# Four graph layers on 32 batches: attention rows spread by DMA through DRAM, and an unmasked attention written as products of exponentials

## The chip, the core and the metric

One core of one Trainium2 chip runs the whole kernel. Its engines are named as in the profile: PE (TensorE, matrix products and transposes), DVE (VectorE), ACT (ScalarE), POOL (GpSimd), SP (SyncE, which here issues nearly all DMAs). PEld is PE's weight load. The metric is the device time of one execution in microseconds (us); the kernel before took 4562.52 us, the median of three runs (4557.34 to 4564.04).

## What is computed

The input x has 32 batches (here called graphs) of 512 nodes with 256 channels, all in float32, and one 512x512 adjacency matrix that they share. Four layers follow each other; each normalizes, applies a ReLU and adds its result to x:

```
h = max(layernorm(x), 0); x = x + L0(h)   # MLP, GAT without a mask, MLP, GAT with the mask
h = max(layernorm(x), 0); x = x + L1(h)   # GAT with the mask and its own node
h = max(layernorm(x), 0); x = x + L2(h)   # transformer block, 8 heads, masked
h = max(layernorm(x), 0); x = x + L3(h)   # GAT with 4 heads, masked

gat(inp, mask, W, a):
    h  = inp @ W
    f1 = h @ a[:F];  f2 = h @ a[F:]
    e  = leaky_relu(f1[:, None] + f2[None, :], 0.2)
    e  = where(mask > 0, e, -9e15)            # left out where there is no mask
    return elu(softmax(e, axis=2) @ h)
```

So there are seven GAT attentions per graph: one without a mask (layer 0, first), and six with it (layer 0, second; layer 1; four heads in layer 3). The change is about how their 512x512 probabilities are made.

## The kernel before

**Tiles.** Nodes or channels lie on 128 partitions; NC = 4 blocks of 128 nodes make 512. A "cell" buffer holds 128 x 1044 floats in SBUF, a "row" buffer 128 x 522, a "page" is a 128 x 1024 buffer in DRAM, a "bank" one of the eight PSUM banks of 128 x 512. "Smalls" are columns of a few floats per partition, one tile for each of the IN_FLIGHT = 6 graphs that may be under way together. There are 31 cells, 9 rows and 72 pages (BUFFERS, L47).

**Attention with a mask** (`gat_probabilities`, L631). The probabilities stand transposed: source node j on the partitions, target node i along the row. `terms` gives each node f2, (1 - alpha) f1 and (alpha - 1) f2. First `rows_ps` (L611, transposes at L617) spreads f2 over all partitions: four PE transposes of a column that is broadcast to 128x128, into one bank. DVE takes from it the largest allowed f2 of each target (four operations, L652). POOL makes of that a shift per target, four small operations at L668 to L674. This shift is a column (node on the partition), and is needed as a row (node along the row, the same on all partitions). `row_of` (L622) does that: four PE transposes into a bank (L617) and a copy on ACT into a row buffer, which also scales it (L627). Two POOL operations add the mask and the shift row into the two cells of p (L687), PE spreads the f1 term (L617 again), four DVE operations join it (L699) and four ACT operations take the exponential (L707).

**Attention without a mask** goes through the same function with no bias: one reduction on DVE (L646), a shift on POOL, `row_of`, no mask addition, four DVE operations that read the shift row (L699), four exponentials (L707). Its sums come from POOL (L1003, L1007) and PE (L1013), their reciprocals from DVE (L1020). `row_of` spreads the reciprocals too (L1021), and DVE multiplies the product of PE (L1030) by that row (L1039).

**Layer 2** turns its probabilities on DVE in 32x32 blocks (L1253) and sends them through DRAM for the rest: a store into a page (L1265) and four loads that put the blocks in their places (L1273), before PE multiplies them (L1286). x and some intermediates are parked in pages as well (L836, fetched at L844).

**The order.** All graphs' operations are written down as a list with an engine, a length in us, a lag (time from the engine's end to the result) and the buffers that they read and write. `Plan.order` (L196) then plays them through on a model of the engines: at each step it takes, on the engine that can start first, the operation with the earliest due time. The due time comes from the graph's number times PERIOD, the operation's distance from the graph's end, and a table of hand-set corrections per operation, SHIFTS (L55 to L85). CLOSE draws the last graphs together. A buffer is taken when the first operation that uses it is placed. The instructions are issued in the resulting order, and each engine, SP among them, runs its own in that order and waits at each for its data. So a waiting DMA issue on SP holds up all DMAs behind it.

Of the kernel before, what the change touches and what calls it, by code (L numbers as in the profile page):

```python
# [16 lines left out]
P = 128  # L17
# [19 lines left out]
TERMS = 3  # L37

# [8 lines left out]
BUFFERS = {"cell": 31, "row": 9, "page": 72}  # L47
# [4 lines left out]
PERIOD = 45.2  # L52
CLOSE = 0.92

SHIFTS = (  # L55
    29, -53, -1, -8, -39, -20, -9, 0, -8, 38, 23, -9, -18, -3, -77, -3, -7, -6, -13, -10, -13,
    -33, -38, -26, -19, -7, -80, -68, -33, -44, 32, -52, -73, -3, -2, -3, -5, -2, 6, -30, 6, 5,
    5, 6, -4, 18, 6, 6, 14, -63, 10, 19, 5, -16, 9, -56, 6, -55, 13, 6, 40, -19, 6, 6, 1, 5, 90,
    5, 5, -152, 3, 44, 5, 5, 1, 0, 1, -19, 1, 0, 0, -2, 0, 0, 2, -104, 0, -1, -24, 0, 8, 77,
    -63, 0, -5, 0, 0, 0, -56, -7, -8, -6, -81, -21, 0, 0, 0, 10, -7, -106, 0, 7, 0, 9, -123, 0,  # L60
    -75, 0, 24, 0, -2, 0, -30, 0, 10, -2, -57, -2, 12, -19, 14, -77, -14, -13, -7, -60, -14,
    -89, 11, 70, -25, 40, 115, 21, -17, -2, 9, 4, -46, -116, -40, -40, -73, -57, -135, -92,
    -106, -76, -169, -150, -145, -58, -212, -66, 3, 3, 3, 3, 3, 25, -13, 80, -111, -19, -25, 5,
    4, 4, 22, 4, 6, 72, 4, 13, -112, 49, -50, -12, 23, 59, 66, 91, 75, 21, -152, 167, 58, 23,
    135, 193, 95, -29, 13, 32, -60, -13, 0, -18, 0, 0, 3, 0, 0, -68, 2, 0, 36, -43, 1, -2, -1,
    0, -5, -11, -7, -6, -51, 3, -5, -60, 0, 23, 0, 27, -104, -73, -114, -225, -216, -123, -155,
    -154, -174, -43, -66, -60, 63, 1, -54, -50, 115, 173, -23, 3, 4, -44, 2, -74, 5, 2, -11,
    -36, 3, -26, -3, 2, 2, -43, 2, 2, -147, 2, 2, -18, 2, 0, 11, -144, 0, 22, 0, 68, 0, 120,
    135, 208, 167, 59, 133, 180, 143, 191, 181, 68, 180, 282, 216, 51, 187, 137, 27, 38, -36,
    -29, -50, -5, 0, -56, -9, 0, -36, 0, 0, 0, 2, 0, -37, -34, -12, -7, 79, -5, 0, 21, -117, 0,  # L70
    -4, -9, 1, -7, 1, -27, 1, -43, 7, -146, -60, -60, -61, 12, -35, -122, -200, -73, -9, -31,
# [279 lines left out]
def adj_preln_kernel(  # L351
# [117 lines left out]
    def held(what, which):  # L469
        return [(what, which)]  # L470
# [10 lines left out]
    class Graph:  # L481
# [140 lines left out]
        def row_of(self, holder, col, dst=(), scale=1.0):  # L622
# [5 lines left out]
            )  # L628
            return r

        def gat_probabilities(self, holder, term, n, bias=None, biasT=None, own=False, after=()):  # L631

# [885 lines left out]
```

## Time and profile before

| what | value |
|---|---|
| median of three runs | 4562.52 us (4557.34 to 4564.04) |
| the profiled execution's own time | 4556.81 us |
| its span, first to last instruction | 4555.0 us |
| instructions in the trace | 72980 |
| mean granted clock of TensorE | 0.974 |
| DMAs: packets, volume, mean rate | 481462, 800.41 MB, 176 GB/s |
| DMA landing, median: 128 KB page load (L1273) | 4.1 us |
| the same, 512 KB page store (L1265, L836) | 3.9 us |
| the same, 512 KB page load (L844) | 5.0 us |
| ACT's first column load at the start (512 elements of 4 B, L410) | 4.7 us |

The page gives each engine's busy time and its share of the span. A group's row names the line, the engine, the operation, what it writes and reads, its form and count, then the busy time in us, the mean length of one in ns, the idle time of the engine just before these instructions, and what ended most of that idle time. Matrix instructions of PE overlap, so the length of one is more than the step from one to the next. A float32 product appears as two instructions; a transpose as one. A view of waits names the waiting engine and line, what it waited for, the total in us, how often, and the longest.

### The profile page before, as it was taken

The numbers are of one execution on the slowest core, as the hardware profiler recorded it, in microseconds if no ns is written. First come the engines' busy times: TensorE is split into PE (matmuls) and PEld (weight loads), VectorE is DVE, ScalarE is ACT, GpSimd is POOL, SyncE is SP. The second block draws the span as 40 slices with busy tenths as digits, with TensorE's granted clock in tenths as the row PEclk, the third lists the DMA queues.
The fourth block names the chain that finished last, engine by engine and source line by source line (L and its number), as shares of the span: only waits on it lengthen the run. The fifth ranks groups of instructions, "written<-read, shape, count | busy, mean of one in ns | idle before, by whom it ended". The sixth has DMA issues, their size and how long they took to land. (4 is left out here: it accounts for less than half of the span.)

```text
span 4555.0 us, 72980 instructions
## 1 busy us (share of the span) xinstructions
PE 4328.2 (95%) x22288; PEld 2698.2 (59%) x22288; DVE 3570.2 (78%) x8824; ACT 3110.0 (68%) x6501; POOL 2992.2 (66%) x3055
## 2 busy tenths in 40 slices
PE   8999999999999999999999999999999999999865
PEld 5666666566666566566566666666665656565432
DVE  4576888787888787888887888788788877888864
ACT  4566677677677677677677677777776676677653
POOL 2334766766776766776766776766776666667768
PEclk9999999999999999999999999999999999999977
DMA  3365656555656555656555656555565565565760
GB/s 108 98 190 182 206 168 198 181 176 167 198 182 185 180 182 163 197 182 184 181 183 164 196 185 190 180 187 161 190 194 173 179 194 177 158 198 191 218 184 19
DMA packets 481462, 800.41 MB, mean 176 GB/s; under 512 B 50608, under 2 KB 364464, under 8 KB 481072
## 3 DMA queue, kind: packets, MB, share of 16 engines
q1 hardware_dynamic: 479456, 795.74, 56.3%
q8 instruction: 180, 2.95, 0.3%
q14 instruction: 210, 1.72, 0.1%
q10 hardware_dynamic: 1616, 0.01, 0.0%
HBM read 409.67 MB, written 385.88 MB: 175 GB/s over the span
## 5 line engine op out<-in xcount | busy, mean ns | idle before, releaser
L1243 ACT ACTIVATE cell<-cell,smalls 128x512 f32<-128x512 f32 x1024 | 732.6, 716 | 302.9 <-DVE smalls L1235 293.6
L687 POOL TENSOR_TENSOR cell<-mask_biasT,row 128x1024 f32<-128x1024 bf16 x320 | 683.7, 2149 | 259.6 <-ACT row L627 239.1
L1235 DVE CUSTOM_DVE_ANT_0 cell<-bank,mask_bias 128x512 f32<-128x512 f32 x1024 | 683.4, 674 | 124.8 <-PE bank L1216 121.7
L1253 DVE STREAM_TRANSPOSE cell<-cell 128x512 f32<-128x512 f32 x1024 | 696.8, 696 | 43.8 <-ACT cell L1243 34.5
L652 DVE CUSTOM_DVE_ANT_0 masked<-bank,mask_bias 128x512 f32<-128x512 f32 x768 | 520.5, 678 | 88.4 <-PE bank L617 80.0
L707 ACT ACTIVATE cell<-cell,smalls 128x512 f32<-128x512 f32 x640 | 440.3, 716 | 102.9 <-DVE cell L699 99.7
L794 PE MATMUL bank<-cell,cell 128*128 128x260 f32 x2048 | 478.1, 385 | 4.7 <-ACT cell L707 3.3
L580 PE MATMUL bank<-cell,mlp_sb 128*128 128x512 f32 x1024 | 469.0, 596 | 4.1 <-DVE cell L1168 1.4
L601 PE MATMUL bank<-fc_sb,cell 128*128 128x256 f32 (+1 forms) x2048 | 471.4, 381 | 1.3 <-DVE cell L1077 1.3
L537 ACT ACTIVATE cell<-cell,smalls 128x256 f32<-128x256 f32 x768 | 421.9, 591 | 67.9 <-POOL smalls L530 57.3
L1030 PE MATMUL bank<-cell,cell 128*128 128x512 f32 x1024 | 464.6, 599 | 2.9 <-DVE smalls L1235 2.9
L794 PEld LDWEIGHTS bank<-cell,cell 128*128 128x128 f32 x2048 | 383.8, 190 | 121.8 <-issue 32.6
L601 PEld LDWEIGHTS bank<-fc_sb,cell 128*128 128x128 f32 x2048 | 381.0, 189 | 82.1 <-DVE cell L813 15.9
L1286 PE MATMUL bank<-cell,cell 128*32 128x256 f32 x4096 | 329.0, 423 | 97.0 <-DMA cell<-page 61.2
L617 PEld LDWEIGHTS bank<-ident,smalls 128*128 128x128 f32 x2304 | 266.6, 139 | 215.4 <-issue 62.7
L699 DVE SCALAR_TENSOR_TENSOR cell<-bank,smalls,cell 128x512 f32<-128x512 f32 x512 | 363.4, 737 | 30.5 <-POOL cell L687 29.5
L520 DVE BATCH_NORM_STATS2 smalls<-cell 128x6 f32<-128x256 f32 x768 | 315.1, 410 | 77.0 <-POOL cell L1093 55.1
L617 PE MATMUL bank<-ident,smalls 128*128 128x128 f32 x2304 | 346.5, 281 | 29.0 <-POOL smalls L674 21.1
L763 DVE SCALAR_TENSOR_TENSOR cell<-cell,cell 128x512 f32<-128x512 f32 (+1 forms) x256 | 261.7, 1023 | 136.7 <-ACT cell L754 68.7
L1356 POOL TENSOR_TENSOR cell<-cell,cell 128x1024 f32<-128x1024 f32 x128 | 302.1, 2369 | 84.2 <-DMA page<-cell 24.8
L1046 POOL TENSOR_TENSOR cell<-cell,cell 128x1024 f32<-128x1024 f32 x64 | 151.7, 2370 | 294.4 <-DVE cell L763 166.4
L1093 POOL TENSOR_TENSOR cell<-cell,cell 128x512 f32<-128x512 f32 x192 | 244.1, 1278 | 130.7 <-DMA cell<-page 48.5
(135 smaller groups left out, 8579.3 us busy)
## 6 DMA issues: line engine op xcount, KB each, us to landing
page<-cell SPq DMA_DIRECT2D x704, 512.0 KB, 3.9
cell<-page SPq DMA_DIRECT2D x2048, 128.0 KB, 4.1
cell<-page SPq DMA_DIRECT2D x192, 512.0 KB, 5.0
cell<-in_x_dram SPq DMA_DIRECT2D x64, 512.0 KB, 5.0
out_dram<-cell SPq DMA_DIRECT2D x32, 512.0 KB, 3.0
mlp_sb<-in_L_gnn_mlp_w_dram SPq DMA_DIRECT2D x2, 512.0 KB, 6.4
fc_sb<-in_L_gnn_W_fc_dram SPq DMA_DIRECT2D x1, 1024.0 KB, 6.2
row<-in_adj_dram SPq DMA_DIRECT2D x4, 256.0 KB, 7.0
```

Of the source, the lines that this page charges most:

```text
L537: lambda c=c: act.activation(xn[:, c, :], src[:, c, :], func, bias=off[:, c : c + 1], scale=rstd[:, c : c + 1],),
L580: lambda k=k, s=s, i=i, m=m, mm=mm: pe.matmul(mm.ap, w[:, k, cols + m * P : cols + (m + 1) * P], s[:, i, :], start=(k == 0), stop=(k == nk ...
L601: pe.matmul(mm[:, :n], src[k // 2][:, k % 2, c * P : (c + 1) * P], w[:, k, cols : cols + n], start=(k == 0), stop=(k == nk - 1),)
L617: pe.transpose(bc[:, c * P : (c + 1) * P], col(c).to_broadcast([P, P]), ident)
L652: lambda c=c: dve.tensor_tensor_reduce(masked, f2_ps.ap, bias[:, c, :], 1.0 - ALPHA, FLOOR, op0=ALU.add, op1=ALU.max, accum_out=top[:, c : ...
L687: lambda half=half: pool.tensor_add(p[half].ap, biasT[:, 2 * half : 2 * half + 2, :], w_row[:, None, :].to_broadcast([P, 2, N]),),
L707: lambda j=j, ph=ph, i=i: act.activation(ph[:, i, :], ph[:, i, :], AF.Exp, bias=term(0)[:, j : j + 1]),
L794: pe.matmul(mm[:, :w1], p[j // 2][:, j % 2, c * P : (c + 1) * P], v[:, j, :], start=(j == 0), stop=(j == NC - 1),)
L1030: pe.matmul(mm.ap, h1[jh][:, i, m * P : (m + 1) * P], p[jh][:, i, :], start=(jh + i == 0), stop=(jh + i == 2),)
L1235: lambda h=h, c=c, sc=sc, p=p: dve.tensor_tensor_reduce(p[h // 2][:, h % 2, :], sc[h].ap, mask_bias[:, c, :], -MHA_SCALE, HIGHEST, op0=ALU ...
L1243: lambda h=h, c=c, p=p: act.activation(p[h // 2][:, h % 2, :], p[h // 2][:, h % 2, :], AF.Exp, scale=-1.0, bias=low[:, c, h : h + 1], accu ...
L1253: lambda h=h, c=c, p=p, turned=turned: dve.transpose(turned[h][:, :, :, c % 2, :].rearrange("p l j i -> p j l i"), p[h // 2][:, h % 2, :]. ...
```

## The change

Four things change together.

1. `row_of` is replaced by `row_by_dma`: the column of 128x4 is stored from SBUF into a line of 512 floats in DRAM (one of 32 new "line" buffers), 4 bytes per element, and a second DMA loads this line into all 128 partitions of a row buffer. Both are issued by SP, the second waits for the first to land. It is used for the six masked shifts and for the reciprocals of the open attention. The scale that ACT applied is now applied by POOL to the small column.
2. The attention without a mask no longer adds and then takes exponentials of 128x512. With the lowest term as a reference, three small exponentials (a, e, g) are taken per node, and each probability is, up to a factor per target that the softmax cancels, max(a_i * e_j, g_j): a is spread by PE, and four DVE operations with two scalars each make p. The exponent of a is capped at 40.
3. The planner's lags of DMAs rise (3.4 to 4.2, 3.8 to 4.5), with 5.0 and 4.0 for the two new ones.
4. There are 30 cells instead of 31 and 11 rows instead of 9, and PERIOD, CLOSE and the whole table SHIFTS have other values, so that the order of the instructions on every engine is another one. The planner itself is unchanged.

```diff
-BUFFERS = {"cell": 31, "row": 9, "page": 72}
+BUFFERS = {"cell": 30, "row": 11, "page": 72, "line": 32}
...
-PERIOD = 45.2
-CLOSE = 0.92
+PERIOD = 56.4
+CLOSE = 0.87
 
 SHIFTS = (
...
-        def row_of(self, holder, col, dst=(), scale=1.0):
+        def row_by_dma(self, src, dst=()):
             r = Buffer("row", N)
-            bc = self.rows_ps([holder], col, (), [r, *dst])
-            self.op(
-                "act", 0.6, [bc], [r],
-                lambda: act.activation(r.ap, bc.ap, AF.Copy, scale=scale),
+            line = Buffer("line", N)
+            self.op(
+                "sp", 0.45, [src], [line],
+                lambda: nc.sync.dma_start(
+                    line.ap.rearrange("o (c p) -> p (o c)", p=P), src.ap
+                ),
+                lag=5.0,
+            )
+            self.op(
+                "sp", 0.45, [line], [r, *dst],
+                lambda: nc.sync.dma_start(
+                    r.ap,
+                    bass.AP(tensor=line.ap.tensor, offset=line.ap.offset, ap=[[0, P], [1, N]]),
+                ),
+                lag=4.0,
             )
             return r
 
+        def open_probabilities(self, f):
+            low_ps = self.rows_ps([f], lambda c: f[:, c : c + 1, 2])
+            low = self.small("low", 1)
...
+                lambda: dve.tensor_reduce(
+                    low.ap, low_ps.ap, axis=mybir.AxisListType.X, op=ALU.min
+                ),
...
+                dve.tensor_scalar(
+                    a.ap, f[:, :, 1], low[:, :1], MOST, op0=ALU.subtract, op1=ALU.min
+                )
+                dve.tensor_scalar(d.ap, f[:, :, 2], low[:, :1], None, op0=ALU.subtract)
...
+                act.activation(a.ap, a.ap, AF.Exp)
+                act.activation(e.ap, d.ap, AF.Exp, scale=-1.0 / (1.0 - ALPHA))
+                act.activation(g.ap, d.ap, AF.Exp, scale=-ALPHA / (1.0 - ALPHA))
...
+            p = [Buffer("cell", 2, N) for _ in range(2)]
+            a_ps = self.rows_ps([a], lambda c: a[:, c : c + 1], [e, g], [q for q in p])
+            for j in range(NC):
...
+                    lambda j=j, ph=ph, i=i: dve.tensor_scalar(
+                        ph[:, i, :], a_ps.ap, e[:, j : j + 1], g[:, j : j + 1],
+                        op0=ALU.mult, op1=ALU.max,
+                    ),
...
                 pool.tensor_add(w.ap, t, term(1))
-                pool.tensor_scalar(
-                    w.ap, w.ap, 0.0, (1.0 - ALPHA) / ALPHA, op0=ALU.max, op1=ALU.mult
-                )
+                pool.tensor_scalar(w.ap, w.ap, 0.0, -1.0, op0=ALU.max, op1=ALU.mult)
+                pool.tensor_scalar(t, t, -ALPHA / (1.0 - ALPHA), None, op0=ALU.mult)
                 pool.tensor_add(w.ap, w.ap, t)
...
-            w_row = self.row_of(w, lambda c: w[:, c : c + 1], p, -ALPHA / (1.0 - ALPHA))
+            w_row = self.row_by_dma(w)
...
-            p, _ = self.gat_probabilities([f], lambda t: f[:, :, t], 0)
+            p = self.open_probabilities(f)
...
-            rinv_row = self.row_of(rinv, lambda c: rinv[:, c : c + 1])
+            rinv_row = self.row_by_dma(rinv)
```

## The prediction

> **What bounds the kernel now.** I read the busy shares first, then the span by stages, then who waits for whom, and last the rows of the operations that go.
>
> ```profile
> PE 4328.2 (95%) x22288; PEld 2698.2 (59%) x22288; DVE 3570.2 (78%) x8824; ACT 3110.0 (68%) x6501; POOL 2992.2 (66%) x3055
> ...
> q1 hardware_dynamic: 479456, 795.74, 56.3%
> ```
>
> TensorE (PE) is busy 95% of the span; the next engine, VectorE (DVE), 78%. The view by windows (columns: length, then busy time of PE, weight loads, DVE, ACT, POOL, granted clock, DMA share, GB/s) shows where PE idles:
>
> ```profile
> 2000.00:3000.00 1000.00, 979.48 (x5138) 616.27 (x5136) 819.06 (x2012) 714.73 (x1497) 685.51 (x698) 0.99 0.58 181
> ...
> 4214.00:4328.00 114.00, 94.57 (x528) 49.95 (x528) 97.58 (x253) 76.30 (x170) 85.51 (x78) 0.91 0.72 218
> 4328.00:4442.00 114.00, 76.20 (x387) 42.75 (x386) 75.47 (x190) 57.70 (x130) 77.78 (x78) 0.79 0.63 183
> 4442.00:4555.00 113.00, 63.32 (x229) 32.33 (x227) 50.68 (x110) 43.24 (x74) 90.42 (x78) 0.73 0.06 19
> ```
>
> In the middle PE idles about 20 us in 1000. In the last 341 us (the drain, where the last graphs run out) it idles 107 us and POOL leads at the end. So up to 4214 us the time is PE's instruction stream: what leaves PE there leaves the time, if the other engines still feed it. PE's own waits, and SP's (the queue of all these DMAs):
>
> ```profile
> PE bank L1286 <- DMA cell<-page: 61.2, 42, 3.1
> PE bank L617 <- POOL smalls L674: 21.1, 12, 4.2
> ...
> SPq L1273 <- DMA page<-cell: 410.9, 222, 5.4
> ```
>
> PE waits little for any one thing; the most for pages that layer 2 sends through DRAM. Then the operations that go or slow down:
>
> ```profile
> L617 PE MATMUL bank<-ident,smalls 128*128 128x128 f32 x2304 | 346.5, 281 | 29.0 <-POOL smalls L674 21.1 <-DVE smalls L1020 3.2 <-DVE smalls L652 2.4
> L627 ACT ACTIVATE row<-bank 128x512 f32<-128x512 f32 x256 | 151.2, 592 | 91.7 <-PE bank L617 88.9
> L687 POOL TENSOR_TENSOR cell<-mask_biasT,row 128x1024 f32<-128x1024 bf16 x320 | 683.7, 2149 | 259.6 <-ACT row L627 239.1 <-DMA cell<-page 8.7 <-DVE cell L1039 6.7
> ```
>
> and, from the timeline of PE, a run of eight transposes and a run of four:
>
> ```profile
> 1000.18 1.04 PE L617 MATMUL bank<-ident,smalls 128*128 128x128 f32 x8
> ...
> 1100.59 0.60 PE L617 MATMUL bank<-ident,smalls 128*128 128x128 f32 x4
> ```
>
> **Step 1, PE.** The built order holds 1280 transposes from smalls at this line where it held 2304: 1024 fewer (per graph: four for each of six masked shift rows, four for the reciprocal row, four for the open attention's shift). A transpose's own 281 ns overlaps its neighbours; in the stream, four more cost 1.04 - 0.60 = 0.44 us, 0.11 each. The page's row gives 346.5/2304 = 0.15, neighbours included. I take 0.12, nearer the run: 1024 x 0.12 = 123 us (113 to 154). Of PE's busy time 234 of 4328 us lies in the drain, where PE doesn't set the end, so 94.6% counts: **-116 us** (-107 to -146). The Trainium skill ("TensorE: Matmul & The Clock Gate", Part 4: PE-mode transpose) puts a 128x128 transpose in one kernel's context at about 275 ns, which agrees with the row's 281; used as a price per transpose it would make 282 us. The two timeline rows show that this is a latency, and not the step.
>
> **Step 2, a wait that goes.** PE waited 21.1 us for shifts from POOL (L674) and 3.2 us for the reciprocals (L1020), to spread them. Both instructions are gone. What stands behind them may be late next, so I take half: **-12 us** (0 to -24).
>
> **Step 3, ACT, DVE, POOL.** ACT loses 256 copies (151 us) and 128 exponentials of 716 ns (92 us), and gains 96 of 128x4 (the 128x12 row took 180 ns: 17 us). DVE keeps 128 operations of 128x512 from PSUM in the open attention (730 ns before; two scalars in place of a row), and gains 64 of 128x4 (at 180 ns, the 128x4 reciprocal: 12 us). POOL gains 64 of 128x4 (some 240 ns: 15 us). None sets the middle: 0, hidden under PE, which has over 160 us in 1000 more work than DVE.
>
> **Step 4, the rows' new path.** Before: four transposes and a copy, 0.6 + 0.59 us, 1.3 with the hops. After: a store of 512 elements of 4 B to DRAM and a broadcast load of 256 KB. No row here stores 4 B elements. The nearest is the first column load (512 elements of 4 B from DRAM, on ACT's queue): 4.7 us to landing; the 512 KB page stores take 3.9, and the slowest DMA of the start-up 9.3. I take 4.7, the same count of elements. The load lies between the 128 KB (4.1) and 512 KB rows (5.0): 4.4. Together 9.1 us, 8 more than before. The Trainium skill ("DMA: Bandwidth & Descriptors", Rules for kernel authors) speaks against the store: a last dimension that isn't contiguous becomes one descriptor per element, and should be rearranged. It gives no price for this; the column load agrees that such a transfer is slow for its 2 KB, no run shows the store, and by the rule at its worst the sum is that of the rival on SP below.
>
> The consumer is POOL's mask addition (L687), and behind it on POOL stand the other additions. In the new order the POOL work between a shift and its addition adds up, by the rows' durations, to under 9.5 us for 105 of 192 rows, 463 us short in all; POOL idles 1563 us. Before, POOL idled 249 us for these rows, and PE's weight loads waited 8.2 + 4.1 + 2.8 = 15 us for L687. In proportion 15 x 463/249 = 28: **+13 us**. Ends: 0 (POOL's idle time hides it), and +79, if the 92.1 us that DVE waited for L687 grow alike and all reach PE. The reciprocal rows are covered: between reciprocal and first use the new order has some 16 us of DVE work (8 before), short of 9.5 us once.
>
> **Step 5, SP and the DMA engines.** SP issues 448 more DMAs, at some 0.4 us 180 us; it issues for about 1240 us of 4555 now, so this hides. The wait that is added is the load's for its store, with all of SP's queue behind it. In the new order 86 of 224 pairs have no more than one issue between, so SP stands still there. Directly behind the 224 loads stand another shift's DMA 106 times, layer 2's pages 77 times, and parked x pages. But the same order moves layer 2's own stores and loads apart: 14 of 512 have at most one issue between where 139 had, 7.3 on average where it was 4.1. So 100 close pairs stand where 139 stood. The DMA engines get busier: 28,672 packets of 2 KB at the mean 86 ns of a packet (56.3% x 16 x 4555/479,456) are 3.4% of the span, and 114,688 of 4 B between 1.4% (9 ns, the packet time of the column loads in the trace) and 13.5% (86 ns): from 56% to 61-73%. PE's waits for pages at L1286 are 61.2 us, 87 with the weight loads'. Wider spacing and busier engines pull opposite ways: **0**, between -87 (all gone) and +87 (doubled).
>
> **Step 6, the drain.** The last addition of layer 1 (own mask) starts at 4231.5 us, so the drain holds little but layers 2 and 3. Layer 3's first row is 8 us later, the other heads' rows come while POOL works: **+8 us** (0 to +16, two graphs).
>
> **Sum.** -116 - 12 + 13 + 0 + 8 = -107: span 4555 - 107 = 4448; with the 1.8 us around it (4556.8 measured) 4450; the median of the runs stands 5.7 us above the profiled one: **4455 us**.
>
> **Rivals.** (a) *SP becomes the bound: slower.* Now 411 us of SP's waiting for page stores go with 87 us of PE's waiting for pages, 0.21 to one. The 107 us gained are used up by 510 us more of SP's waiting: 2.3 us per pair if all 224 wait, 5.9 if only the 86 close ones do. So it decides from a store that lands after 7 to 10.6 us rather than 4.7. At 11 us and all pairs: 224 x 6.3 x 0.21 = 296 us, 4750; the close ones alone: 114, 4570; between, **4660**. For: nothing here shows the store, and single page loads took 8.8 us. Against: the column loads' 4.7. (b) *The other engines take half back.* DVE has 819 us of 1000; on a span shorter by 2.5% 840, in order, with ACT waiting 294 us for it (L1243 <- L1235). If PE's idle time in the middle grows from 22 to 35 us in 1000: 13 x 3.9 = 50, **4505**. For: buffers fall from 31 to 30. Against: ACT is freed of 226 us. (c) *The new order mends pages and drain too:* half of the 87, and a third of the drain's 107 us: 4455 - 43 - 36 = **4376**. That the change does not do what it says is excluded for the counts by the built order.
>
> **How the numbers follow.** About 0.2% (9 us) is what a measurement here can tell from no change. Forecast (4400 to 4505) 0.60; (b) (4505 to 4553) 0.17; (c) and below 0.07; so faster 0.84; same 0.05; (a) and like it, slower, 0.11. The steps' ends, taken as independent, reach 94 us down (30, 12, 13, 87, 8 squared and added) and 111 up (9, 12, 66, 87, 8): 4361 to 4566. 8 in 10 lie within **4365 to 4550**, leaving some 0.04 below, 0.16 above.
>
> **What would show it.** Step 1: some 1800 transposes in place of 2816 in all, PE busy near 4205, PE share still about 94-95%. Step 2: no PE wait for L674. Step 4: line<-smalls landing near 4.7 us and row<-line near 4.4, POOL waiting some 460 us for rows. Step 5: PE's wait at layer 2's product (L1286) near 87 us, DMA share 61-73%. Step 6: PE idle in the last 341 us near 115. I am wrong if the stores land after 7 us and PE's waits for pages grow past 190 us (rival a), if PE's share falls under 93.5% in the middle with DVE or ACT behind its waits (rival b), or if the transposes' step was not 0.12 us.

## The result, and the profile after

The changed kernel took 5977.02 us (median of four runs, 5950.70 to 5983.38), the kernel before on the same chip 4560.27 (4557.34 to 4564.04). The ratio is 1.3095 (95% interval 1.3054 to 1.3136): 31% slower, where 2.4% faster was forecast.

First the page of the kernel after: busy shares, the granted clock by slices, the large DMA queue and two groups.

```profile
PE 4538.0 (76%) x21264; PEld 2736.7 (46%) x21264; DVE 3589.0 (60%) x8888; ACT 2906.0 (49%) x6213; POOL 3042.2 (51%) x3119
...
PEclk8998898888888888988888888889888998988877
...
q1 hardware_dynamic: 629984, 854.95, 66.5%
...
L730 POOL TENSOR_TENSOR cell<-mask_biasT,row 128x1024 f32<-128x1024 bf16 x320 | 681.9, 2145 | 899.5 <-DMA row<-line 741.8
...
L581 PE MATMUL bank<-cell,mlp_sb 128*128 128x512 f32 x1024 | 495.2, 612 | 12.5 <-POOL cell L1088 7.0
```

The last group in the page of the kernel before:

```profile
L580 PE MATMUL bank<-cell,mlp_sb 128*128 128x512 f32 x1024 | 469.0, 596 | 4.1 <-DVE cell L1168 1.4
```

The 1024 instructions are gone from PE, and yet it is busy for 4538 us where it was 4328; no engine is busy for more than 76% of the span. So nothing became a bound by its work: everything waits. The mean granted clock fell from 0.974 to 0.871, and the products that are the same as before take longer (612 ns where it was 596).

The view by windows of the kernel after, for the same millisecond as before and for the last 341 us:

```profile
2000.00:3000.00 1000.00, 762.78 (x3631) 460.47 (x3630) 604.58 (x1491) 499.50 (x1063) 534.75 (x531) 0.88 0.69 145
...
5634.00:5975.00 341.00, 179.35 (x802) 86.28 (x800) 168.81 (x399) 126.75 (x261) 206.85 (x199) 0.74 0.49 105
```

The loss lies in the steady middle: PE idles 237 us of 1000 (20 before). The DMA engines' share rose from 0.58 to 0.69, but they move less: 145 GB/s where it was 181. Busier and slower at once means that packets stand in the engines. In the packet records the mean packet of 4 KB takes 278 ns (178 before; the median is 159 in both), and 6036 packets of 512 B or more took over 1 us (209 before). The row stores' own packets look harmless: of the 172465 packets of 4 B all but 64 took under 1 us, 12 ns in the mean, as before. What stands is other DMAs' packets, of 4 KB (4062 over 1 us, 54 before) and of 1 KB (1423, 33 before).

Who waits for whom in the kernel after (engine and line, what it waited for, total us, times, longest), first all engines, then SP's own queue:

```profile
POOL cell L730 <- DMA row<-line: 985.6, 117, 27.4
...
PE bank L1328 <- DMA cell<-page: 372.7, 87, 16.0
...
PEld bank L1328 <- DMA cell<-page: 235.7, 73, 12.5
```

```profile
SPq L635 <- DMA line<-smalls: 914.8, 119, 15.3
...
SPq L1315 <- DMA page<-cell: 385.7, 255, 12.1
```

All of the waits shown end in a DMA. (PE also waits 230 us for a maximum of DVE, L700, and 216 us for ACT, L1341; what stood behind those was not followed.) POOL waits 986 us for the new rows, PE's wait for pages grew from 61 to 373 us (its weight loads' from 26 to 236), and SP stands 915 us at the loads of rows (L635) until their stores (L628) have landed. In the 86 pairs with at most one issue between, the load is issued 10.4 us after its store (median; 7.9 to 14.2).

What lies in those 10 us? The queue of SP in one such stretch of the kernel after, by its timeline, and the DMA view of 1932 to 1952 us, whose two rows stand in 40 slices of half a microsecond (busy tenths, GB/s):

```profile
1933.52 0.32 SPq L878 DMA_DIRECT2D page<-cell  x1
1934.22 0.37 SPq L628 DMA_DIRECT2D line<-smalls  x1
1938.93 0.32 SPq L1307 DMA_DIRECT2D page<-cell  x1
1946.17 0.32 SPq L635 DMA_DIRECT2D row<-line  x1
```

```profile
DMA  0000399700000005999500030401201344999950
GB/s 0 0 0 0 139 401 369 143 1 0 0 0 0 0 0 229 401 139 41 8 0 0 8 16 16 41 41 33 74 16 57 147 156 67 305 386 205 25 8 0
```

The row's store is issued at 1934.22. The page store issued just ahead of it runs at up to 401 GB/s, then the engines are empty until the next page store (1938.93) moves its part. The row store's own 4 B packets are done by 1936.5, at 7 to 9 ns each; the page store's packets behind them take up to 5.4 us. From 1941 to 1946 no slice passes 41 GB/s; then the row's load is let go. One picture proves little, since the queue itself waits here. So I averaged over all 224 stores: packets of 512 B or more that start in each microsecond after a store's issue. "Unread" marks kernels, told of below, whose stores no instruction reads. Rows without stores count from the DMA issue ahead of the place where the compared kernel has its store.

| us after the issue | -2 | 0 | 2 | 4 | 6 | 7 | 8 | 10 | 12 | 14 |
|---|---|---|---|---|---|---|---|---|---|---|
| kernel after | 90 | 93 | 96 | 60 | 25 | 15 | 16 | 30 | 76 | 113 |
| e11, unread | 103 | 91 | 86 | 64 | 34 | 23 | 23 | 46 | 94 | 87 |
| e3, e11's places, no stores | 134 | 131 | 130 | 121 | 112 | 123 | 112 | 105 | 98 | 101 |
| e18, unread | 138 | 174 | 71 | 52 | 14 | 17 | 23 | 43 | 70 | 71 |
| before, e18's places, no stores | 149 | 199 | 131 | 88 | 59 | 66 | 88 | 96 | 59 | 61 |
| e2, unread | 87 | 71 | 46 | 32 | 15 | 11 | 11 | 34 | 51 | 52 |
| e13, e2 with elements 512 B apart | 87 | 67 | 45 | 84 | 47 | 42 | 57 | 86 | 68 | 92 |

Some 5 to 10 us after a store the traffic of all DMAs falls to about a fifth, whether the line is read or not. Without the stores, in the same order of instructions, it does not fall like that; nor does it in e13, where the same 512 elements go to addresses 512 B apart. The comparison within one order is needed: in the order of e1 and e2 the traffic thins out at these places even with no stores (e1: 26 packets at 7 us; 22 in e16, whose reads cost nothing).

### The profile page after: what moved, and what is told of

Same layout as the page of the kernel before. It is cut to its first block, busy times and chain, and to the rows that moved or that the text cites. A ratio compares the mean times of both kernels' runs of the same rounds, so it can differ in the third digit from the quotient of the medians.

```text
span 5975.4 us, 71173 instructions
## 1 busy us (share of the span) xinstructions
PE 4538.0 (76%) x21264; PEld 2736.7 (46%) x21264; DVE 3589.0 (60%) x8888; ACT 2906.0 (49%) x6213; POOL 3042.2 (51%) x3119
## 3 DMA queue, kind: packets, MB, share of 16 engines
q1 hardware_dynamic: 629984, 854.95, 66.5%
## 5 line engine op out<-in xcount | busy, mean ns | idle before, releaser
L730 POOL TENSOR_TENSOR cell<-mask_biasT,row 128x1024 f32<-128x1024 bf16 x320 | 681.9, 2145 | 899.5 <-DMA row<-line 741.8
L1285 ACT ACTIVATE cell<-cell,smalls 128x512 f32<-128x512 f32 x1024 | 733.4, 716 | 662.9 <-DVE smalls L1277 660.7
L1328 PE MATMUL bank<-cell,cell 128*32 128x256 f32 x4096 | 448.6, 492 | 443.8 <-DMA cell<-page 372.7
L700 DVE CUSTOM_DVE_ANT_0 masked<-bank,mask_bias 128x512 f32<-128x512 f32 x768 | 520.8, 678 | 93.3 <-PE bank L618 74.9
L1328 PEld LDWEIGHTS bank<-cell,cell 128*32 128x32 f32 x4096 | 223.9, 134 | 674.3 <-issue 327.4
L792 ACT ACTIVATE cell<-cell 128x512 f32<-128x512 f32 (+1 forms) x256 | 187.3, 732 | 682.9 <-DMA page<-cell 398.5
L581 PE MATMUL bank<-cell,mlp_sb 128*128 128x512 f32 x1024 | 495.2, 612 | 12.5 <-POOL cell L1088 7.0
L602 PE MATMUL bank<-fc_sb,cell 128*128 128x256 f32 (+1 forms) x2048 | 491.8, 392 | 16.9 <-ACT cell L592 11.4
L1072 PE MATMUL bank<-cell,cell 128*128 128x512 f32 x1024 | 484.9, 616 | 0.0
L749 ACT ACTIVATE cell<-cell,smalls 128x512 f32<-128x512 f32 x512 | 352.4, 716 | 243.0 <-DVE cell L741 235.0
L1258 PE MATMUL bank<-cell,cell 32*128 32x512 f32 x2048 | 355.7, 700 | 150.1 <-ACT cell L590 133.1
L602 PE MATMUL bank<-l_sb,cell 128*128 128x268 f32 (+1 forms) x1024 | 280.8, 422 | 248.6 <-DVE smalls L700 230.2
L602 PEld LDWEIGHTS bank<-l_sb,cell 128*128 128x128 f32 x1024 | 204.7, 206 | 329.8 <-DVE smalls L700 252.6
```

The costliest lines, as they stand in the source:

```text
L581: lambda k=k, s=s, i=i, m=m, mm=mm: pe.matmul(mm.ap, w[:, k, cols + m * P : cols + (m + 1) * P], s[:, i, :], start=(k == 0), stop=(k == nk ...
L602: pe.matmul(mm[:, :n], src[k // 2][:, k % 2, c * P : (c + 1) * P], w[:, k, cols : cols + n], start=(k == 0), stop=(k == nk - 1),)
L700: lambda c=c: dve.tensor_tensor_reduce(masked, f2_ps.ap, bias[:, c, :], 1.0 - ALPHA, FLOOR, op0=ALU.add, op1=ALU.max, accum_out=top[:, c : ...
L730: lambda half=half: pool.tensor_add(p[half].ap, biasT[:, 2 * half : 2 * half + 2, :], w_row[:, None, :].to_broadcast([P, 2, N]),),
L1072: pe.matmul(mm.ap, h1[jh][:, i, m * P : (m + 1) * P], p[jh][:, i, :], start=(jh + i == 0), stop=(jh + i == 2),)
L1285: lambda h=h, c=c, p=p: act.activation(p[h // 2][:, h % 2, :], p[h // 2][:, h % 2, :], AF.Exp, scale=-1.0, bias=low[:, c, h : h + 1], accu ...
```

## The experiments

On the chips used here the kernel before took 4532.73 to 4540.19 us (median for each set; 4560.27 on the chip of the result). Most kernels were run once, and no difference under 100 us is read from those; five have intervals. The expectations name their theories by letters. The main ones are that the stores stop the traffic, that the new order of the instructions costs the time, and, later, that writes into neighbouring addresses wait for each other.

**Stores, loads or order?** e1 makes the rows by PE and ACT again, in the changed kernel with its new table of due times:

```diff
-            line = Buffer("line", N)
+            bc = self.rows_ps([src], lambda c: src[:, c : c + 1], (), [r, *dst])
             self.op(
-                "sp", 0.45, [src], [line],
...
-                "sp", 0.45, [line], [r, *dst],
...
+                "act", 0.6, [bc], [r],
+                lambda: act.activation(r.ap, bc.ap, AF.Copy),
             )
```

> The changed kernel, with the rows spread by PE and ACT again (four transposes and a copy); open attention, planner constants and SHIFTS as changed. Theory S (each store of 512 elements of 4 B stops the traffic of the DMA engines for some 6.5 us; 224 of them make the 1415 us): without stores the loss goes, 4450 to 4650 us. Theory T (the store's late landing holds SP's queue and the consumers, other traffic unharmed): the same. Theory O (the new order is bad by itself): stays over 5500 us.

4861.79 us (before: 4532.73). 1115 us of the loss go with the rows' path, and 329 stay without any of its DMAs: between the ranges of theories S and O, inside neither.

e2 is e1 with the 224 stores put beside, read by nobody (against the changed kernel; `extra` keeps the table of due times in step):

```diff
+            bc = self.rows_ps([src], lambda c: src[:, c : c + 1], (), [r, *dst])
...
             line = Buffer("line", N)
...
-                lag=5.0,
...
+                lag=5.0, extra=True,
```

> As e1, and the 224 stores of 512 elements of 4 B are issued as well, into lines that nobody reads; no broadcast loads. Nothing waits for the stores but the reuse of a line 32 rows later. Theory S: the stores alone cost the time, 5700 to 6000 us. Theory T: within 150 us of e1. In between, shares of both.

5392.58 us: 531 more than e1, for 224 DMAs of 2 KB whose data nobody wants. That is more than theory T allows and less than S expected. The wait views, first of e1, then of e2:

```profile
PE bank L1317 <- DMA cell<-page: 64.5, 41, 4.6
```

```profile
PE bank L1329 <- DMA cell<-page: 268.5, 102, 14.4
```

PE waits four times as long for pages that have nothing to do with the stores.

e3 keeps the new path's loads and takes the stores out. Each row is loaded from one of two fixed lines (all shifts -30, all reciprocals 1/512), so its output isn't the reference's.

```diff
+            self.op("sp", 0.45, [src], [line], lambda: None, lag=5.0)
...
-                    bass.AP(tensor=line.ap.tensor, offset=line.ap.offset, ap=[[0, P], [1, N]]),
+                    bass.AP(
+                        tensor=fixed_lines[fixed].tensor, offset=fixed_lines[fixed].offset,
+                        ap=[[0, P], [1, N]],
+                    ),
```

> The changed kernel without its 224 stores: every row is loaded by the broadcast DMA from one of two lines that are filled once at the start, so shifts and shares are constants and the output is another one. Theory S: 4400 to 4650 us. A rival B (128 reads of the same 2 KB by all engines are what stops the traffic): 5500 us or more. Theory T: like S, as no load waits for a store.

4677.29 us: 1300 below the changed kernel, with the same sequence of instructions on PE and on SP (the stores apart), and still 145 above the kernel before. Rival B, the reads, is out (5500 us or more). Later e11 put the stores back into e3, unread (the loads still take the fixed lines, so the output is e3's):

```diff
-            self.op("sp", 0.45, [src], [line], lambda: None, lag=5.0)
+            self.op(
+                "sp", 0.45, [src], [line],
+                lambda: nc.sync.dma_start(
+                    line.ap.rearrange("o (c p) -> p (o c)", p=P), src.ap
+                ),
+                lag=5.0,
+            )
```

> e3 (rows loaded from two fixed lines, so another output) with the 224 stores of 512 elements of 4 B issued as well, unread. The stop without anybody waiting for the stores: by e2 over e1, 4677 + 531 = 5200 us. If the stop alone made all of the loss: 5900 us. What lies between this run and the changed kernel is the waiting for a store's landing, on SP and for the rows.

5722.07 us, between the two sums expected: the stores alone cost 1045 of the 1300 us. No load waits for a store here, and yet the rows come late. The wait views and the windows, first of e3, then of e11:

```profile
POOL cell L733 <- DMA row<-shift_line: 287.8, 76, 9.6
```

```profile
2000.00:3000.00 1000.00, 936.12 (x4733) 576.61 (x4732) 786.86 (x1974) 640.81 (x1373) 685.35 (x701) 0.97 0.66 193
```

```profile
POOL cell L739 <- DMA row<-shift_line: 950.4, 114, 24.3
```

```profile
2000.00:3000.00 1000.00, 778.17 (x3720) 476.46 (x3723) 621.58 (x1541) 501.08 (x1079) 527.17 (x544) 0.88 0.71 151
```

With the stores POOL waits 950 us for loads that are free to start, at 151 GB/s instead of 193, and PE falls from 936 us of 1000 to 778, near the changed kernel's 763. The wait that a load has for its store is worth the rest: 5977 - 5722 = 255 us. SP does not go free of the unread stores, though. Its DMAs take eight semaphores in turn (438 to 440 issues each in e11's trace), and an issue waits for the DMA that had its semaphore before. So SP's waits in e11 name the stores for 272 us, most of it here:

```profile
SPq L1324 <- DMA line<-smalls: 194.9, 75, 7.2
```

In e2 they name them for 44 us, in e18 for 32, and the stores cost 531 and 711 us there. So these waits are not what the stores cost.

e18 asks the same of the kernel before, with its own order untouched: 224 unread stores, issued by SP where the copies of the rows stand.

```diff
+                act.activation(r.ap, bc.ap, AF.Copy, scale=scale)
+                if stored:
+                    line = lines.pop(0)
+                    lines.append(line)
+                    nc.sync.dma_start(line.rearrange("o (c p) -> p (o c)", p=P), holder.ap)
```

> The kernel before in its own order, rows by PE and ACT, with the 224 stores of 512 neighbouring elements of 4 B issued by SP at the place of the copy, into 32 lines that nobody reads. Theory S, the price in an order that fits: between e2 - e1 and e11 - e3, 531 to 1045 us over before: 5070 to 5590. If the price needs a disturbed order: under 4800 us.

5247.07 us where before took 4536.37: 711 us for the same 224 stores, with the other instructions of every engine in before's sequence. So the price is that of the stores, and depends on the surroundings (531, 711, 1045).

**A queue's trouble or everybody's?** e7 issues the stores on ACT's queue instead of SP's:

```diff
-                lambda: nc.sync.dma_start(
+                lambda: nc.scalar.dma_start(
                     line.ap.rearrange("o (c p) -> p (o c)", p=P), src.ap
```

> The changed kernel, the 224 stores issued by ACT on its own queue at the same places of the order. Theory S1 (a store stops the DMA engines for every queue): 5700 to 6100 us. Theory S2 (it stops only what stands behind it in the rings of its own queue, and SP): 4700 to 5200 us, and the 4 KB packets take as long as in e3 (181 ns) and not as in the changed kernel (278 ns).

6034.28 us, no better than 5977.02; packets of 4 KB still take 241 ns. Another queue doesn't help.

**What about the stores?** Four forms of the DMA, in e2's surroundings or in the changed kernel. e4 writes the line in the order of the partitions, so that each partition's four floats are one run of 16 B (128 runs); POOL and DVE then read the row with a stride.

```diff
-                    line.ap.rearrange("o (c p) -> p (o c)", p=P), src.ap
+                    line.ap.rearrange("o (p c) -> p (o c)", p=P), src.ap
```

> The changed kernel, with the line in the column's own order: 128 runs of 16 B instead of 512 of 4 B, the same 2 KB; POOL and DVE read the row with a step of four elements. Theory S with a cost per run: the stop shrinks to a quarter, 1415/4 = 350 us stay, 4800 to 4950 us. Theory S with a cost per store whatever its runs: 5800 to 6000 us.

4848.48 us. Its DMA view gives the landing that the page of the changed kernel lacks:

```profile
row<-line SPq DMA_DIRECT2D x224, 256.0 KB, 4.2
...
line<-smalls SPq DMA_DIRECT2D x224, 2.0 KB, 4.0
```

The same bytes by the same path land in 4.0 us, traffic doesn't stop (packets of 4 KB: 182 ns), and 1129 us are back. A part of what is left is the price of the strided reading: POOL's addition (L730) takes 2651 ns instead of 2145, 320 times.

e13 is e2 with each element at least 512 B from any other (a line is now a buffer of 128 x 4 x 128 floats, of which every 128th is written):

```diff
-                    line.ap.rearrange("o (c p) -> p (o c)", p=P), src.ap
+                    line[:, :, 0], src.ap
```

> e2 (rows by PE, unread stores of 512 elements of 4 B: 5393 us, 531 over e1), but each element goes 512 B away from the next in DRAM, so that no two share a block of that size. Theory R (writes of 4 B to neighbouring addresses wait for each other): the loss shrinks, under 5000 us. Theory C (each element costs, wherever it goes): 5300 to 5450 us.

e14 is e2 with one column of 128 neighbouring elements:

```diff
-                    line.ap.rearrange("o (c p) -> p (o c)", p=P), src.ap
+                    line[:, :P].rearrange("o (c p) -> p (o c)", p=P), src[:, :1]
```

> e2, but each store writes one column, 128 elements of 4 B side by side, instead of four. Theory C: a quarter of the 531 us or less stays, up to 5000 us (e4's 128 runs of 16 B cost 171 us over e3). A cost per store: 5300 to 5450 us.

e16 is e2 with 512 reads of 4 B from DRAM in place of the stores:

```diff
-                    line.ap.rearrange("o (c p) -> p (o c)", p=P), src.ap
+                    columns[:, line.slot, :], full_line.rearrange("o (c p) -> p (o c)", p=P)
```

> e2, but the 224 extra DMAs go the other way: 512 elements of 4 B read from a line in DRAM into a scratch column of 128x4 that nobody uses, the form of the column loads at the start that the forecast priced the store by. Theory W (only writes of such elements stop the traffic): 4850 to 4950 us, near e1. If reads cost the same: 5300 to 5450 us.

| kernel | what 224 DMAs do | time | over e1 | mean 4 KB packet |
|---|---|---|---|---|
| e1 | none | 4861.79 | | 180 ns |
| e2 | 512 stores of 4 B, side by side | 5392.58 | +531 | 267 ns |
| e14 | 128 stores of 4 B, side by side | 5221.96 | +360 | 229 ns |
| e13 | 512 stores of 4 B, 512 B apart | 4868.12 | +6 | 181 ns |
| e16 | 512 reads of 4 B, side by side | 4868.93 | +7 | 180 ns |

e14 lies between its two expectations. The DMA views, of e13 and of e16:

```profile
line<-smalls SPq DMA_DIRECT2D x224, 2.0 KB, 2.3
```

```profile
columns<-full_line SPq DMA_DIRECT2D x224, 2.0 KB, 3.7
```

Neither the number of elements nor their size is dear: 512 stores of 4 B land in 2.3 us when they lie apart, and as reads they land in 3.7. Dear are writes of single elements to neighbouring addresses, and a quarter of the elements keeps two thirds of the price. The Trainium skill ("DMA: Bandwidth & Descriptors", Specifications) says that below 512 B a transfer is done as read-modify-write. If that were a price for each element, e13 would pay it in full, and it paid nothing that shows; neighbours that wait for each other's read-modify-write would fit e2, e13, e14 and e16, but no run here shows that mechanism, nor the size of the block that they would share (e4's runs of 16 B are neighbours too). e13 also spreads a line over 256 KB where e2 has 2 KB; no run separates distance from area.

**The order.** e5 is e1 in before's order: its PERIOD, CLOSE, buffers and lags, and its SHIFTS without the five entries of the operations that the open attention lost. e6 does that with the full change.

```diff
-BUFFERS = {"cell": 30, "row": 11, "page": 72, "line": 32}
+BUFFERS = {"cell": 31, "row": 9, "page": 72, "line": 32}
...
-PERIOD = 56.4
-CLOSE = 0.87
+PERIOD = 45.2
+CLOSE = 0.92
```

> e1 with the order of before: PERIOD, CLOSE, BUFFERS, lags and SHIFTS of before, less the five entries of the operations that the open attention no longer has. So it is the kernel before with the open attention alone changed (128 transposes, 128 exponentials of 128x512 fewer). Theory O2 (of the 330 us by which e1 is over before, the new order makes nearly all, as it was laid out for other rows): 4450 to 4560 us. Rival P (the open attention costs them): 4750 to 4900 us.

> The changed kernel, stores and loads and all, with the order of before as in e5. If the stores set the time whatever the order (theory S): 5700 to 6300 us. If the new order were a good part of the loss with these rows too: under 5500 us.

e5: 4890.60 us against 4535.19, ratio 1.0782 (1.0765 to 1.0800). e6: 6055.56 us. The old table didn't bring the old time back. e5 lies just where rival P had it, and yet it did not tell apart what I had hoped it would: with five operations gone, the planner lays another order from the same table (e10, below, speaks against P). e6 shows that the new order isn't what costs 1400 us. That leaves e1's 329 us, and two kernels were made for it. e12 is the kernel before with nothing but the planner's DMA lags changed (3.4 to 4.2, 3.8 to 4.5); the instructions are the same, their order isn't.

> The kernel before, instruction for instruction the same work, with the planner's lags of DMAs as in the change (3.4 to 4.2, 3.8 to 4.5): only the order differs. Theory F: an order that is laid anew without fitted SHIFTS loses 100 to 400 us: 4640 to 4940. Rival: the order matters little: 4520 to 4600 us.

4750.14 us, 213 more for the same instructions (the windows of e12):

```profile
2000.00:3000.00 1000.00, 959.64 (x4978) 598.39 (x4970) 802.70 (x1969) 689.84 (x1459) 668.20 (x679) 0.99 0.59 180
```

e10 is the kernel before in exactly its own order, with the open attention's instructions exchanged at their places: the products of exponentials stand where the sums and exponentials stood, and operations that are no longer needed issue nothing.

```diff
-            p, _ = self.gat_probabilities([f], lambda t: f[:, :, t], 0)
+            p = self.open_in_place(f)
...
+            self.op("pe", 0.47, [low], [bank, r, *p], lambda: None)
...
+                self.op("act", 0.72, [f, ph.part(i)], [ph.part(i)], lambda: None)
```

> The kernel before in exactly its own order of instructions, with the open attention's instructions alone exchanged at their places (4 transposes and 4 exponentials of 128x512 fewer per graph, 128 each in all). Theory F (e5's loss of 355 us comes from an order that the planner lays anew and that no longer fits): the saved transposes, 128 x 0.12 = 15 us, and nothing else: 4500 to 4540 us beside 4535. Rival P (the open attention itself is slow): 4750 us or more.

4540.36 us against 4537.03, ratio 1.0007 (0.9998 to 1.0017). So the new open attention by itself costs nothing and brings nothing, though PE loses 128 transposes by it and ACT 160 operations of 128x512 (it gains 96 small ones). A table of due times belongs to one list of operations: laid anew for another list, or from other lags, it lost 213 us (e12) to 355 us (e5). How much of e3's 145 us is the order and how much the loads, no run separates.

**What is a transpose worth?** e15 is the kernel before in its own order; of the four transposes for each of 192 masked shift rows one is kept and its result replaced by the constant -30. A constant shift cancels in the softmax; the guard against overflow is gone.

```diff
-            w_row = self.row_of(w, lambda c: w[:, c : c + 1], p, -ALPHA / (1.0 - ALPHA))
+                    lambda: pe.transpose(bc[:, :P], w[:, :1].to_broadcast([P, P]), ident),
...
+                        AF.Identity, bias=lowered, scale=0.0,
```

> The kernel before in its own order, with one transpose instead of four for each of the 192 masked shift rows and a constant shift of -30 written by the same ACT instruction (so another output): 576 transposes fewer, nothing else moved. The forecast's step 1 (PE's stream sets the time, 0.12 us each, 94.6% of it counts): 65 us less, 4460 to 4480 us. Rival N (the time is not handed on, as in e10): within 15 us of before.

4518.25 us against 4540.19, ratio 0.9944 (0.9924 to 0.9965). The page of e15, then its groups view with the 576 fewer transposes (before: 2304):

```profile
PE 4288.0 (95%) x21712; PEld 2631.5 (58%) x21712; DVE 3566.3 (79%) x8825; ACT 3117.7 (69%) x6501; POOL 2990.4 (66%) x3055
```

```profile
L619 PE MATMUL bank<-ident,smalls 128*128 128x128 f32 x1536 | 244.5, 284 | 10.1 <-DVE smalls L1038 3.2 <-DVE smalls L654 2.7 <-ACT smalls L1013 1.7
...
L687 PE MATMUL bank<-ident,smalls 128*128 128x128 f32 x192 | 55.4, 290 | 21.5 <-POOL smalls L676 21.5
```

By Step 1's price they should have brought 576 x 0.12 x 94.6% = 65 us. They brought 22, a third (16 to 35 by the interval). PE's own busy time fell by 40 us (from 4328.2; roughly, as the two traces come from different chips), 0.07 us for each. The edit isn't quite pure: ACT's instruction for a row takes 680 ns where it took 592.

**Versions that might beat both.** e9 turns the column on PE first (one transpose of 128x4 to 4x128, a small ACT copy) and stores four runs of 512 B; e8 is the same in before's order.

```diff
+            self.op(
+                "pe", 0.15, [src], [tp, flat],
+                lambda: pe.transpose(tp[:NC, :P], src.ap, ident), extra=True,
+            )
+            self.op(
+                "act", 0.25, [tp], [flat],
+                lambda: act.activation(flat[:NC, :], tp[:NC, :P], AF.Copy), extra=True,
+            )
...
-                    line.ap.rearrange("o (c p) -> p (o c)", p=P), src.ap
+                    line.ap.rearrange("o (c p) -> (o c) p", p=P), flat[:NC, :]
```

> The changed kernel with its own new order; the column is first turned to 4x128 by one PE transpose and an ACT copy, and the store writes 4 runs of 512 B instead of 512 of 4 B. Theory S: as e4 and e3, no stop: 4650 to 4850 us. If any round trip through DRAM per row cost as much: over 5500 us.

> As e6, but the column of 128x4 is first turned to 4x128 by one PE transpose and copied by ACT (4 partitions), so that the store writes 4 runs of 512 B. 224 more transposes than the changed kernel, 800 fewer than before. Theory S: no stop, so the time is the order's: 4400 to 4600 us, under before if the old order suits the later rows, up to 100 us over it if the 9 us of two DMAs come late in that order. If any store and load through DRAM costs as much: over 5000 us.

e9: 4814.72 us; in close pairs the load is issued 2.8 us after the store. e8: 5221.64 us, ratio 1.1509 (1.1490 to 1.1528), far above what was expected. POOL waits 196 us for rows in e8 and 148 in e9, which doesn't account for the 407 us between them; what does stays open. A stop of the traffic it is not: packets of 4 KB take 177 ns in e8 (178 before). Both are slower than before.

e17 is the kernel before in its own order with e10's open attention, and with no shift rows at all: -30 is folded into the mask once, and the spread of f2, its maxima, the shift rows and POOL's additions of mask and shift go. As in e15, the constant cancels and the guard against overflow is gone, so it suits inputs like these alone.

```diff
-            q, _ = self.gat_probabilities(
+            q, _ = self.fixed_shift(
...
+                    for t in (mask_biasT, self_biasT):
+                        pool.tensor_scalar(t[:, j, :], t[:, j, :], -30.0, None, op0=ALU.add)
```

> The kernel before in its own order, with the open attention of the change in place (e10) and the masked shifts left out: a constant shift of -30, which the softmax cancels, is folded into the mask, so the f2 rows, the maxima, the shift rows and POOL's mask additions all go (192 rows: 1536 transposes, 768 DVE operations of 678 ns, 384 POOL additions of 2149 ns, 192 copies). The guard against an overflow goes with them: this holds for these inputs only. By e15's rate (22 us for 576 transposes): 1536 x 0.038 = 60 us, 4480. By the forecast's step 1: 1536 x 0.12 x 0.946 = 174 us, 4365. With the stalls that end as well: down to 4300.

4446.03 us against 4536.37, ratio 0.9808 (0.9791 to 0.9824), the fastest kernel of this study. The page of e17:

```profile
PE 4163.5 (94%) x20624; PEld 2532.2 (57%) x20624; DVE 3103.5 (70%) x7320; ACT 2916.6 (66%) x6245; POOL 2034.4 (46%) x1975
```

PE has 1664 instructions fewer, DVE 467 us less work and POOL 958 us less, and the time falls by 90 us. The forecast for the whole change was 107.

## Why the prediction was wrong, step by step

The way from the kernel before to the kernel after, in one look each (before: 4533 on e1's and e3's chip, after on the chip of the result):

| from | to | difference | what it is |
|---|---|---|---|
| before 4533 | e3 4677 | +145 | new order, loads of rows, PE's and ACT's savings |
| e3 4677 | e11 5722 | +1045 | the stores all but stop the DMA traffic; nobody reads them |
| e11 5722 | after 5977 | +255 | rows and SP wait until the stores land |

**The step that failed is the store's price**, in Step 4 (4.7 us to landing) and Step 5 (the stores' effect on other DMAs, at 0, ends -87 and +87). The store lands after some 10.4 us, and while it does, everybody's traffic falls to a fifth. I had taken the price from the nearest row, the column *loads* of 512 x 4 B. e16 shows that row to be sound for reads (3.7 us, no loss) and to say nothing of writes. A landing was also the wrong quantity to price: e18 loses 711 us with stores that nobody reads, and SP's waits name them for 32 us. Step 5 had counted the stores' packets, and these were as short as its low end said (9 ns; 12 in the mean over all packets of 4 B); what it put at nothing is what they do to the packets of other DMAs.

**Rival (a)** had the sign and the deciding point: the landing of some 10.4 us lies past the 7 us, and PE's waits for pages passed the 190 us, that the text gave as the sign. Its price was too small by far, 4570 to 4750 at 11 us. It took 0.21 us of PE's time for each us of SP's waiting. By that price the waits of SP shown above come to (914.8 + 385.7 - 410.9) x 0.21 = 187 us, 13% of the loss of 1417. The queue's wait is only what SP sees; the stop reaches each load already issued, whoever issued it (e7, e11, e18). The range missed by 1427 us, since its upper end let PE's waits for pages no more than double and gave the stores no other way to act.

**Step 1.** The count was right: 1280 transposes at this line. Their worth was not. In before's own order, 576 fewer brought a third of their price (e15), 128 fewer nothing that can be told (e10). A share of 95% on PE did not mean that what leaves its stream leaves the time: e17 takes 165 us from PE's busy time and 90 from the kernel's; which waits took the place of the rest, no run shows. The step of 0.12 us may have been too long as well: in e15 PE's busy time fell by some 0.07 us for each. But e3, with 1024 out, has 66 us less even at a lower clock (0.955), so that stays open.

PE's busy time, forecast near 4205, rose to 4538 (4262 in e3, without the stores), mainly because a PE that waits is granted less clock. The clock records hold two values, 1.0 and 0.5, and a product of L581 takes 596 ns at 1.0 and 1029 at 0.5. PE was busy at 0.5 for 762 us (174 before); by these two lengths that makes some 250 of the 333 us, an estimate. In the trace of after PE has 147 gaps of over 3.4 us, 1205 us in all (before: 9 gaps, 42 us), and 135 of the 160 stretches at 0.5 begin in such a gap or within 1.5 us of its end (before: 6 of 41, so not every one has such a gap). The Trainium skill ("TensorE: Matmul & The Clock Gate", HAM oscillation) puts the throttling behind gaps of about that length; the kernel after agrees with it.

**Step 2** was right about the wait that goes (its 12 us can't be read by themselves), and its warning too: no PE wait for the shift's POOL instructions is left, and what is late next is the row itself, at POOL (985.6 us).

**Step 3** was about right. Forecast: ACT 226 us less, DVE 12 and POOL 15 more; measured 204 less, 19 and 50 more.

**Step 4, the rest.** The load (4.4 us) was well sized: 4.2 us in e4, and 5.4 in e3 for the shifts. POOL's waiting (forecast near 460 us) was 288 us in e3 without stores, 986 with them. What PE would feel of it, 28 us of waits by its weight loads where 15 were, came to 30 us in the kernel after and 8 in e3; DVE's wait for these additions, 92 us before, came to 356 and 86. PE's own waits were sized about right; DVE's, which the text let grow to 171 us at the upper end, went far beyond it.

**Step 5's** count of close pairs was right, and its DMA share (61 to 73%; measured 66.5% on the large queue, 61.8% in e3) in part for a wrong reason: on a span that is 31% longer, more packets at the old length would have made a smaller share; packets that stand made the rest. SP's issues took 1441 us by the trace of before, not 1240; nothing hangs on it.

**Step 6.** PE idles 162 us in the last 341 (forecast 115, before 107). The stores lie there too, so the 8 us can't be separated.

**Without the stores' fault** the forecast would have failed as well: e3 is 145 us slower than before, not 107 faster. PE's waits in e3:

```profile
PE bank L1331 <- DMA cell<-page: 99.3, 44, 5.2
PE bank L1352 <- ACT row L1344: 94.0, 26, 6.9
PE bank L559 <- ACT cell L544: 66.0, 18, 12.8
```

The order that I credited with spacing layer 2's pages apart left PE waiting 99.3 us for pages, where before had 61.2. Rival (c) has nothing for it. Rival (b), the other engines, has its sign nearly: PE's share in the middle is 93.6% (the text said under 93.5%), and ACT stands behind 218 us of PE's idle time, where it was 59. But it isn't the fuller engines that (b) had in mind: in the middle DVE and ACT were less busy in e3 (787 and 641 us of 1000) than before (819 and 715). ACT came later, it did not have more to do.

## What to carry to other kernels

Price a DMA by a row of the same direction and the same pattern of addresses, and ask not only when it lands but what other DMAs do meanwhile; where no such row exists, its cost has no upper end that the page can give. Never store a column to DRAM element by element into neighbouring addresses: runs of 16 B, elements spread apart, or a turn on PE before the store, did not stop the traffic here. And measure a removed instruction's worth by taking it out in place: a planned order laid anew cost 213 us for the same instructions (e12). Even in place it can be worth less than its step: a PE that was busy 95% of the span gave back a third of the forecast price.

## What the runs showed of the hardware that was not expected

- 512 stores of 4 B side by side, in one DMA of 2 KB, cut all DMA traffic of the core to about a fifth for some microseconds (23 packets per us in e11 where e3 has 112 to 123) and landed after about 10 us; 224 of them cost 531 to 1045 us. In the stretch shown their own packets took 7 to 9 ns each; it is the packets of another DMA behind them that stood, for up to 5.4 us. The same elements 512 B apart landed in 2.3 us and cost nothing that shows; 128 runs of 16 B landed in 4.0 us.
- It isn't the queue: issued by ACT the stores cost as much (6034 us against 5977).
- The granted clock of TensorE has two values in these traces, 1.0 and 0.5, and the same product took 596 ns and 1029 ns at them (kernel after).
- A POOL addition of 128x1024 that reads a row with a stride of four floats took 2651 ns instead of 2145.
